# Bilinear feature interaction on one core: w in four loads of 128 rows, x in 16 KB pieces, and another set of x blocks on fifteen DMA engines

## The chip, the core and the metric

The kernel runs on one core of a Trainium2 chip. The core has a matrix engine (TensorE, PE in the profile; its weight loads are PEld), a vector engine (DVE), a scalar engine (ACT), a general engine (GpSimd, POOL) and a queue engine that only issues transfers (SyncE, SP). Sixteen DMA engines move data between the core's memory and HBM for all of them. The metric is the device time of one execution in microseconds (us). Lower is better.

## The reference

Each of 4096 samples has 32 fields of 64 numbers. For each of the 496 pairs of fields i < j, field i is multiplied by the pair's own 64 x 64 matrix, and the result by field j, element by element:

```python
B, F, D = (4096, 32, 64)
idx_i, idx_j = np.triu_indices(F, k=1)
vi = inputs[:, idx_i, :]
vj = inputs[:, idx_j, :]
vidots = jnp.einsum('bpd,pde->bpe', vi, W)
return vidots * vj            # (4096, 496, 64) float32
```

The output has 520 MB, the input x 33.6 MB and the weights W 8.1 MB, so nearly all traffic is the output.

## The kernel before

**Tiling.** The samples form 16 blocks of 256. A block's x lies in one tile `xs`: 128 partitions, each with two samples (k = 0 and 1) of 32 x 64 floats, 8 KB a sample. Half a block (128 samples, one k) is a unit t of work, 32 in all. The pairs are cut into five groups (`bounds`, L45), and one output tile `ot` holds one unit's results of one group, 2880 to 3360 KB. There are three `ot` buffers (`opool`, L58), two `xs` buffers (`xpool`, L55) and four PSUM buffers.

**Steps.** For a unit, `turn_x` (L148) transposes eight fields at a time on PE, and ACT copies them out of PSUM in three pieces (L158 to L160). For each i, up to 16 pairs are one step: two matmuls, one for each half of the columns (L254), then a multiply with field j into `ot`, on DVE straight from PSUM (L274), or, for the seven i in `aside` (L49), a copy by ACT (L271) and the multiply on POOL (L272). When a group is full, SP issues the output transfer (L279). The first three units go through the groups together (`LEAD`, L178), later units one after the other.

**Weights.** W is loaded as it lies, one pair to a partition (16 KB), in the parts `wrows` (L51, L52): 128, 128, 128 and 112 pairs. `order_w` (L130) reorders a quarter of a part (DVE, for part 2 POOL, for half of part 3 ACT), `turn_w` (L139) transposes it, and the result lies in a tile `wT`: one for the first three parts, one for the last (`home_of`, L114). Parts 0 and 1 are loaded into `ot` buffers, part 2 into its own place in `wT`, part 3 into the later home of part 3. A step whose pairs lie across the border of the two homes has its matmuls split there (L250).

**Loads.** SP issues, in this order: half of block 0, w parts 0 and 1, the other half of block 0, block 1, w parts 2 and 3 (L205 to L213). After that SP's queue carries outputs alone. Block b + 1 is loaded while block b is worked on (`loads`, L202). A plain load (`load_x`) is one transfer from ACT's queue. Every third block (3, 6, 9, 12, 15; L231) goes from GpSimd's queue instead, through `load_fifteen` (L95): first 120 of the 128 partitions in one transfer, then the other 8 partitions in two transfers of half the fields each. GpSimd's queue gives a transfer of few rows to a run of DMA engines that starts where the one before ended; `turn_engines` (L86) are tiny transfers that move this start: by 5 at the beginning, by 1 between the parts of each such load, by 11 at the end. So 120 partitions go to fifteen engines, always the same fifteen, and the 8 + 8 pieces of the rest to all sixteen once.

**Layout of xs.** `new_x` (L69) leaves 16 floats between the two samples of a partition, so that every x transfer moves pieces of 8 KB.

Of the kernel before, what the change touches and what calls it, by code (L numbers as in the profile page):

```python
# [8 lines left out]
F32 = mybir.dt.float32  # L9
# [3 lines left out]
def kernel(  # L13
# [16 lines left out]
    nc = tc.nc  # L30

    B, F, D = x.shape
    P = 128
    NB = 2
    assert 2 * D == P and B % (NB * P) == 0
    NBLK = B // (NB * P)
    NP = F * (F - 1) // 2
# [10 lines left out]

    aside = (1, 3, 5, 7, 9, 11, 13)  # L49

    cuts = [*range(0, NP, P), NP]  # L51
    wrows = list(zip(cuts[:-1], cuts[1:]))  # L52

    const = ctx.enter_context(tc.tile_pool(name="const", bufs=1))
    xpool = ctx.enter_context(tc.tile_pool(name="xpool", bufs=2))  # L55
# [8 lines left out]
    xs = {}  # L64

    def rows_of(dram: bass.AP, blk: int) -> bass.AP:
        return dram[blk * NB * P : (blk + 1) * NB * P]

    def new_x(blk: int):  # L69

        wide = xpool.tile([P, NB, F * D + 16], F32, tag="xs", name=f"xs_{blk}")
        xs[blk] = wide[:, :, : F * D].rearrange("p k (f d) -> p k f d", d=D)

    def load_x(blk: int, eng, k0: int = 0, k1: int = NB):
        src = rows_of(x, blk).rearrange("(p k) f d -> p k f d", k=NB)
        eng.dma_start(out=xs[blk][:, k0:k1], in_=src[:, k0:k1])
# [18 lines left out]
    def load_fifteen(blk: int):  # L95
        rows = rows_of(x, blk).rearrange("(p k) f d -> p k f d", k=NB)
        dst = xs[blk]

        def part(ps: slice, fs: slice):
            tc.keep_in_program_order(nc.gpsimd.dma_start(out=dst[ps, :, fs, :], in_=rows[ps, :, fs, :]))  # L100

        part(slice(0, SWR), slice(0, F))
        turn_engines(1)
        for h in range(2):
            part(slice(SWR, P), slice(h * F // 2, (h + 1) * F // 2))


    wflat = w.rearrange("p d e -> p (d e)")
    raw, wT = {}, {}
    EU = 2 * BANK // P  # L110
    NU = E2 // EU


    def home_of(c: int):  # L114
        home, tag, n = (wrows[3][0], "w3", NP - wrows[3][0]) if c == 3 else (0, "w", wrows[3][0])
        if home not in wT:
            wT[home] = const.tile([P, n, E2], F32, tag=tag, name=f"wT_{home}")
        return wT[home][:, wrows[c][0] - home : wrows[c][1] - home, :]

    def load_w(c: int):  # L120

        a, b = wrows[c]
        if c == 2:
            raw[c] = home_of(c).rearrange("p r e -> p (r e)")
        else:
            pool, tag = (const, "w3") if c == 3 else (opool, "ot")
            raw[c] = pool.tile([P, D * D], F32, tag=tag, name=f"raw_{c}")
        nc.sync.dma_start(out=raw[c][: b - a, :], in_=wflat[a:b])  # L128

    def order_w(c: int, k: int, copy):  # L130
        r = wrows[c][1] - wrows[c][0]
        rp = tpool.tile([P, EU, 2, D], F32, tag="tmp", name=f"rp_{c}_{k}")
        src = raw[c][:r, :].rearrange("p (d h e) -> p e h d", h=2, d=D)
        ins = copy(rp[:r], src[:, k * EU : (k + 1) * EU])  # L134
        if c > 0:
            tc.keep_in_program_order(ins)
        return rp

    def turn_w(c: int, k: int, rp, copy):  # L139
        r = wrows[c][1] - wrows[c][0]  # L140
        pt = psum.tile([P, EU, P], F32, tag="ps", name=f"ptw_{c}_{k}")
        for n in range(EU):
            nc.tensor.transpose(  # L143
                pt[:, n, :r], rp[:r, n].rearrange("p h d -> p (h d)"), ident[:r, :r]
            )
        copy(home_of(c)[:, :, k * EU : (k + 1) * EU], pt[:, :, :r].rearrange("p e r -> p r e"))  # L146

    def turn_x(blk: int, k: int, q: int, copy):  # L148


        pt = psum.tile([P, RUN // 2, P], F32, tag="ps", name=f"ptx_{blk}_{k}_{q}")
        for u in range(RUN // 2):
            f = q * RUN + 2 * u
            nc.tensor.transpose(  # L154
                pt[:, u, :], xs[blk][:, k, f : f + 2, :].rearrange("p f d -> p (f d)"), ident
            )
        xT = xtpool.tile([P, 2, RUN // 2, P], F32, tag="xT", name=f"xT_{blk}_{k}_{q}")
        copy(xT[:, 0], pt)  # L158
        copy(xT[D:, 1], pt[:D])  # L159
        copy(xT[:D, 1], pt[D:])  # L160
        return xT
# [40 lines left out]
    loads = {place[blk * NB, LATE]: blk + 1 for blk in range(2, NBLK - 1)}  # L202
    loads[place[LEAD, LATE]] = 2

    new_x(0)  # L205
    load_x(0, nc.sync, 0, 1)
    load_w(0)
    load_w(1)
    load_x(0, nc.sync, 1, NB)
    new_x(1)  # L210
    load_x(1, nc.sync)
    load_w(2)
    load_w(3)  # L213
    turn_engines(5)

    v, p, a = nc.vector.tensor_copy, nc.gpsimd.tensor_copy, nc.scalar.copy
# [5 lines left out]
    for k, copy in ((0, a), (3, a), (1, v), (2, a)):  # L222
        turn_w(0, k, rps.pop((0, k)), copy)

    ots = {}
    for s, (t, st) in enumerate(sched):
        blk, kt = divmod(t, NB)
        g, i, c0, m = steps[st]
        if s in loads:
            new_x(loads[s])  # L230
            if loads[s] % 3 == 0:  # L231
                load_fifteen(loads[s])
            else:
                load_x(loads[s], nc.scalar)
        for what, *args in due.get(s, ()):
            if what == "x":
                xT[tuple(args)] = turn_x(*args, a)
            elif what == "turn":
                turn_w(*args, rps.pop(tuple(args)), a)
            else:  # L240
                c, k = args
                rps[c, k] = order_w(c, k, ((v, v, p, v), (v, v, p, a))[k % 2][c])

        base, end = groups[g]
        pa = p0[i] + c0
        if pa == base:
            ots[t] = opool.tile([P, cap, D], F32, tag="ot", name=f"ot_{t}_{g}")
        ot = ots[t]
        ps = psum.tile([P, 2, CH, E2], F32, tag="ps", name=f"ps_{s}")
        for lo, hi in ((0, wrows[3][0]), wrows[3]):  # L250
            home, lo, hi = lo, max(pa, lo), min(pa + m, hi)
            if lo < hi:
                for h in range(2):
                    nc.tensor.matmul(  # L254
                        ps[:, h, lo - pa : hi - pa, :],
                        xT[blk, kt, i // RUN][h * D : (h + 1) * D, (i + h) % 2, i % RUN // 2, :],
                        wT[home][h * D : (h + 1) * D, lo - home : hi - home, :],
                        start=True,
                        stop=True,
                    )  # L260
        o = pa - base
        j = i + 1 + c0
        dst = ot[:, o : o + m, :].rearrange("p m (h e) -> p m h e", h=2)
        src = ps[:, :, :m, :].rearrange("p h m e -> p m h e")
        xj = xs[blk][:, kt, j : j + m, :].rearrange("p m (h e) -> p m h e", h=2)
        if i in aside and c0 == 0:

            tmp = dst
            if t >= LEAD:
                tmp = tpool.tile([P, CH, 2, E2], F32, tag="tmp", name=f"tmp_{s}")  # L270
            nc.scalar.copy(tmp, src)  # L271
            nc.gpsimd.tensor_mul(dst, tmp, xj)  # L272
        else:
            nc.vector.tensor_mul(dst, src, xj)  # L274

        ends = (p0[2], end) if s < NS and (t, g) == (0, 0) else (end,)
        if pa + m in ends:
            n0 = p0[2] if len(ends) > 1 and pa + m == end else base
            nc.sync.dma_start(  # L279
                out=rows_of(out, blk).rearrange("(p k) n d -> p k n d", k=NB)[:, kt, n0 : pa + m, :],  # L280
                in_=ot[:, n0 - base : pa + m - base, :],
            )
# [28 lines left out]
```

## Time and profile before

| | |
|---|---|
| time, median of 3 | 1338.6 us (1338.33 to 1338.76) |
| span of the profiled execution | 1337.1 us |
| HBM read, written | 41.68 MB, 520.09 MB |
| DMA queue of SP / ACT / GpSimd | 532.43 / 18.87 / 10.50 MB |
| share of 16 engines' time, same order | 93.9% / 3.4% / 2.0% |
| output transfers | 161, median 15.6 to 17.0 us from issue to landing by size (most of them) |
| x, plain, from ACT: 9 | 25.4 us from issue to landing |
| x, 120 rows, from GpSimd: 5 | 24.8 us |
| x, 8 rows, from GpSimd: 10 | 28.2 us |
| last part of w, 112 rows: 1 | 30.3 us |
| DVE waits for an output buffer | 210.7 us in 101 waits, longest 5.5 |
| POOL waits for an output buffer | 173.9 us in 65 waits, longest 5.3 |

The time from issue to landing contains the time in the queue behind earlier transfers. An engine that waits for an `ot` buffer waits for the landing of the transfer that last read it. DMA shares are the packets' time over the time of all 16 engines, so one busy engine alone has a share of 0.06. A share can come out a little over 1, because a packet is counted where it starts.

### The profile page before, as it was taken

What the parts mean: (1) busy time and instruction counts of PE and PEld (TensorE: products, weight loads), DVE (VectorE), ACT (ScalarE), POOL (GpSimd) and SP (SyncE); (2) the same over time, 40 slices, a digit from 0 to 9 for tenths busy, and PEclk for the clock granted to TensorE, in tenths of its full rate; (3) what the DMA queues carried; (4) which work ended last, traced back from release to release, by engine and by line L of the source; (5) the groups of instructions that cost most, each with busy time, mean ns of one, the idle gap of its engine ahead of it and who ended that gap; (6) DMA issues with size and microseconds to landing.
All of it is one profiled execution on the core that took longest, in us unless ns stands there. A gap on an engine that the chain in (4) does not pass through costs nothing.

```text
span 1337.1 us, 16689 instructions
## 1 busy us (share of the span) xinstructions
PE 1134.5 (85%) x6656; PEld 604.6 (45%) x6656; DVE 952.7 (71%) x1258; ACT 471.4 (35%) x627; POOL 552.4 (41%) x256
## 2 busy tenths in 40 slices
PE   6989898978798897898888898788897979879884
PEld 4555444444444444444444444444444444444442
DVE  5778677766677676776767777577775767767774
ACT  4463333333233333333333333333333323333331
POOL 1752443344334343343453334444344424444431
PEclk9999899989899898998998989899998999989997
DMA  9999999999999999999999999999999999999997
GB/s 371 431 429 425 426 420 429 423 428 431 424 429 420 421 430 423 431 420 427 432 407 430 424 431 425 422 426 405 429 426 428 426 418 427 422 415 430 430 429 318
DMA packets 28894, 562.86 MB, mean 421 GB/s; under 512 B 3536, under 2 KB 3536, under 8 KB 3824
## 3 DMA queue, kind: packets, MB, share of 16 engines
q1 hardware_dynamic: 24304, 532.43, 93.9%
q10 hardware_dynamic: 2448, 18.87, 3.4%
q0 software_dynamic: 2064, 10.50, 2.0%
q8 instruction: 52, 0.85, 0.2%
q14 instruction: 26, 0.21, 0.0%
HBM read 41.68 MB, written 520.09 MB: 420 GB/s over the span
## 4 chain that ended last, share of the span: by engine, by line
DMA 53%; PE 24%; DVE 14%; POOL 4%; issue 2%; ACT 2%; DVEq 0%; SPq 0%; POOLq 0%; ACTq 0%
DMA out_dram<-ot 52%; PE ps L254 22%; DVE ot L274 13%; POOL ot L272 4%; PE ptx L154 2%; DMA xs<-in_r_inputs_dram 1%; PE ptw L143 1%; ACT tmp L271 1%; DVE rp L134 0%; ACT xT L160 0%; ACT xT L158 0%; ACT xT L159 0%; DVEq L274 0%; POOL xs L100 0%; SPq L128 0%
## 5 line engine op out<-in xcount | busy, mean ns | idle before, releaser
L274 DVE TENSOR_TENSOR ot<-ps,xs 128x1024 f32<-128x1024 f32 (+15 forms) x1248 | 937.7, 806 | 353.3 <-DMA out_dram<-ot 210.7
L254 PE MATMUL ps<-wT,xT 64*128 64x512 f32 (+13 forms) x6016 | 1044.8, 488 | 169.3 <-DVE ot L274 164.5
L254 PEld LDWEIGHTS ps<-wT,xT 64*128 64x128 f32 x6016 | 535.1, 196 | 618.9 <-DVE ot L274 372.5
L272 POOL TENSOR_TENSOR ot<-tmp,xs 128x1024 f32<-128x1024 f32 x203 | 478.9, 2359 | 705.7 <-ACT tmp L271 532.5
L271 ACT COPY tmp<-ps 128x1024 f32<-128x1024 f32 x203 | 205.5, 1012 | 475.7 <-PE ps L254 432.5
L158 ACT COPY xT<-ptx 128x512 f32<-128x512 f32 x128 | 74.9, 585 | 322.5 <-PE ptx L154 322.5
L154 PE MATMUL ptx<-ident,xs 128*128 128x128 f32 x512 | 84.4, 288 | 9.7 <-DMA xs<-in_r_inputs_dram 6.5
L154 PEld LDWEIGHTS ptx<-ident,xs 128*128 128x128 f32 x512 | 53.9, 141 | 81.9 <-DVE ot L274 56.3
L160 ACT COPY xT<-ptx 64x512 f32<-64x512 f32 x128 | 74.5, 582 | 1.5
L159 ACT COPY xT<-ptx 64x512 f32<-64x512 f32 x128 | 73.9, 577 | 1.5
L272 POOL TENSOR_TENSOR ot<-ot,xs 128x1024 f32<-128x1024 f32 x21 | 49.8, 2377 | 51.0 <-ACT ot L271 49.9
L271 ACT COPY ot<-ps 128x1024 f32<-128x1024 f32 x21 | 21.3, 1013 | 24.7 <-PE ps L254 17.1
L143 PE MATMUL ptw<-ident,rp 128*128 128x128 f32 (+1 forms) x128 | 18.4, 297 | 5.8 <-DVE rp L134 5.8
L134 DVE COPY rp<-raw 128x1024 f32<-128x1024 f32 (+1 forms) x9 | 14.7, 1653 | 10.7 <-DMA raw<-in_L_rec_W_dram 10.7
L143 PEld LDWEIGHTS ptw<-ident,rp 128*128 128x128 f32 (+1 forms) x128 | 15.6, 155 | 13.8 <-DVE rp L134 5.2
L146 ACT COPY wT<-ptw 128x1024 f32<-128x1024 f32 (+1 forms) x15 | 14.8, 985 | 12.2 <-PE ptw L143 10.9
L100 POOL DMA_DIRECT2D xs<-in_r_inputs_dram x15 | 9.5, 636 | 0.0
L134 POOL COPY rp<-wT 128x1024 f32<-128x1024 f32 x4 | 7.8, 1967 | 0.0
L134 ACT COPY rp<-raw 112x1024 f32<-112x1024 f32 (+1 forms) x3 | 6.0, 1996 | 1.9 <-DMA raw<-in_L_rec_W_dram 1.9
L92 POOL DMA_DIRECT2D scratch<-in_r_inputs_dram x7 | 6.2, 889 | 0.3 <-issue 0.3
L146 DVE COPY wT<-ptw 128x1024 f32<-128x1024 f32 x1 | 1.2, 1223 | 3.1 <-PE ptw L143 3.1
L158 ACT ACT_TABLE_LOAD x1 | 1.3, 1283 | 0.7 <-PEq L298 0.7
(6 smaller groups left out, 0.9 us busy)
## 6 DMA issues: line engine op xcount, KB each, us to landing
out_dram<-ot SPq DMA_DIRECT2D x64, 3360.0 KB, 16.6
out_dram<-ot SPq DMA_DIRECT2D x32, 3168.0 KB, 15.6
out_dram<-ot SPq DMA_DIRECT2D x32, 3104.0 KB, 17.0
out_dram<-ot SPq DMA_DIRECT2D x31, 2880.0 KB, 16.9
xs<-in_r_inputs_dram ACTq DMA_DIRECT2D x9, 2048.0 KB, 25.4
xs<-in_r_inputs_dram POOLq DMA_DIRECT2D x5, 1920.0 KB, 24.8
raw<-in_L_rec_W_dram SPq DMA_DIRECT2D x2, 2048.0 KB, 11.7
xs<-in_r_inputs_dram SPq DMA_DIRECT2D x2, 1024.0 KB, 10.5
```

Source lines behind the costliest of these rows:

```text
L100: tc.keep_in_program_order(nc.gpsimd.dma_start(out=dst[ps, :, fs, :], in_=rows[ps, :, fs, :]))
L134: ins = copy(rp[:r], src[:, k * EU : (k + 1) * EU])
L143: nc.tensor.transpose(pt[:, n, :r], rp[:r, n].rearrange("p h d -> p (h d)"), ident[:r, :r])
L146: copy(home_of(c)[:, :, k * EU : (k + 1) * EU], pt[:, :, :r].rearrange("p e r -> p r e"))
L154: nc.tensor.transpose(pt[:, u, :], xs[blk][:, k, f : f + 2, :].rearrange("p f d -> p (f d)"), ident)
L158: copy(xT[:, 0], pt)
L159: copy(xT[D:, 1], pt[:D])
L160: copy(xT[:D, 1], pt[D:])
L254: nc.tensor.matmul(ps[:, h, lo - pa : hi - pa, :], xT[blk, kt, i // RUN][h * D : (h + 1) * D, (i + h) % 2, i % RUN // 2, :], wT[home][h * ...
L271: nc.scalar.copy(tmp, src)
L272: nc.gpsimd.tensor_mul(dst, tmp, xj)
L274: nc.vector.tensor_mul(dst, src, xj)
```

## The change

It has three parts.

1. *w.* The parts of w are now pairs 0 to 127, 128 to 255, 256 to 367 and 368 to 495, and each is loaded by a transfer of 128 rows; the third carries 16 rows that the fourth loads too. All four transfers then have eight rows for each DMA engine. The 112 wide part is now part 2 (POOL's), and the border of the two homes is at pair 368 instead of 384.
2. *x pieces.* The gap between a partition's two samples is kept only for blocks that go by fifteen engines. In all others the 16 KB of a partition lie together, and the transfer moves one piece for each partition. The first block, loaded half by half, keeps 8 KB pieces.
3. *Which blocks.* Blocks 5, 7, 9, 11, 13, 14 and 15 are loaded by fifteen engines, where 3, 6, 9, 12 and 15 were. Seven loads leave the sixteenth engine out instead of five, and the first comes later.

```diff
-    cuts = [*range(0, NP, P), NP]
+    cuts = [0, P, 2 * P, NP - P, NP]
     wrows = list(zip(cuts[:-1], cuts[1:]))
...
+    fifteen = (5, 7, 9, 11, 13, 14, 15)
+
     def new_x(blk: int):
-
-        wide = xpool.tile([P, NB, F * D + 16], F32, tag="xs", name=f"xs_{blk}")
+        gap = 16 if blk in fifteen else 0
+        wide = xpool.tile([P, NB * (F * D + 16)], F32, tag="xs", name=f"xs_{blk}")
+        wide = wide[:, : NB * (F * D + gap)].rearrange("p (k n) -> p k n", k=NB)
         xs[blk] = wide[:, :, : F * D].rearrange("p k (f d) -> p k f d", d=D)
...
-    def home_of(c: int):
-        home, tag, n = (wrows[3][0], "w3", NP - wrows[3][0]) if c == 3 else (0, "w", wrows[3][0])
+    def home_of(c: int, r: int):
+        home, tag, n = (wrows[3][0], "w3", P) if c == 3 else (0, "w", 3 * P)
...
-        return wT[home][:, wrows[c][0] - home : wrows[c][1] - home, :]
+        return wT[home][:, wrows[c][0] - home : wrows[c][0] - home + r, :]
 
     def load_w(c: int):
 
-        a, b = wrows[c]
+        a = wrows[c][0]
         if c == 2:
-            raw[c] = home_of(c).rearrange("p r e -> p (r e)")
+            raw[c] = home_of(c, P).rearrange("p r e -> p (r e)")
...
-        nc.sync.dma_start(out=raw[c][: b - a, :], in_=wflat[a:b])
+        nc.sync.dma_start(out=raw[c], in_=wflat[a : a + P])
...
-            if loads[s] % 3 == 0:
+            if loads[s] in fifteen:
                 load_fifteen(loads[s])
```

More of the change, by code (lines that the diff above doesn't have):

```diff
@@ L145, in turn_w @@
             )
-        copy(home_of(c)[:, :, k * EU : (k + 1) * EU], pt[:, :, :r].rearrange("p e r -> p r e"))
+        copy(home_of(c, r)[:, :, k * EU : (k + 1) * EU], pt[:, :, :r].rearrange("p e r -> p r e"))
     def turn_x(blk: int, k: int, q: int, copy):
```

## The prediction

> **What bounds the kernel now.** I read the page first: busy shares, DMA row, queues, chain of waits.
>
> ```profile
> PE 1134.5 (85%) x6656; PEld 604.6 (45%) x6656; DVE 952.7 (71%) x1258; ACT 471.4 (35%) x627; POOL 552.4 (41%) x256
> ...
> DMA  9999999999999999999999999999999999999997
> ...
> DMA packets 28894, 562.86 MB, mean 421 GB/s; under 512 B 3536, under 2 KB 3536, under 8 KB 3824
> ...
> DMA 53%; PE 24%; DVE 14%; POOL 4%; issue 2%; ACT 2%; DVEq 0%; SPq 0%; POOLq 0%; ACTq 0%
> ```
>
> No compute engine is above 85%, the DMA row is full in every slice but the last, and over half of the chain that ended last is the output transfer. So the 16 DMA engines are the bound, and the question is whether all 16 work all the time. The view by stretches of time answers it (columns: stretch, length, busy us of PE, PEld, DVE, ACT, POOL, clock, DMA share, GB/s):
>
> ```profile
> 27.00:34.00 7.00, 7.00 (x42) 3.67 (x38) 6.63 (x7) 3.49 (x5) 2.18 (x1) 1.00 1.01 298
> ...
> 1329.00:1331.00 2.00, 0.00 (x0) 0.00 (x0) 0.00 (x0) 0.00 (x0) 0.00 (x0) 0.50 0.06 27
> 1331.00:1333.00 2.00, 0.00 (x0) 0.00 (x0) 0.00 (x0) 0.00 (x0) 0.00 (x0) 0.50 0.06 27
> ```
>
> A share of 0.06 is one engine of 16: after 1329 us a single DMA engine still writes while fifteen have nothing left. The trace also holds the 16 completion events of every transfer, one per engine (the printed views show only the last). In the last output transfer the fifteen land at 1329.2 on average and the last at 1335.35; the span ends 1.75 later. I call this distance (6.2 us here) the **lag**. It is built up, not an accident of the end: from 3.39 us (transfer issued at 1184.2) to 6.56 (issued at 1310.8), a stretch with no x load, so 0.025 us per us. Over a plain x load it hardly moves (4.54 to 4.82 across block 13's, 980.7 to 1011.4). Over a fifteen-engine load it falls: 6.12 to 2.46 (block 6), 6.95 to 3.38 (block 12), 7.00 to 3.39 (block 15). So the engine left out is the lagging one.
>
> The lag also costs time before the end. An output buffer is free when the last engine has landed, there are three of them, and one transfer takes about 7.7 us; at a lag near 7 us the fast engines run dry. The stretches around x loads show it:
>
> ```profile
> 174.00:214.00 40.00, 33.52 (x198) 17.38 (x196) 27.78 (x39) 14.06 (x19) 19.31 (x11) 0.96 1.01 422
> 252.00:292.00 40.00, 32.38 (x184) 17.33 (x186) 26.17 (x37) 12.45 (x17) 14.89 (x7) 0.91 1.01 422
> ...
> 910.00:950.00 40.00, 34.05 (x200) 17.77 (x197) 27.51 (x38) 14.06 (x19) 19.34 (x11) 0.96 0.98 407
> ...
> 1156.00:1196.00 40.00, 33.66 (x198) 17.38 (x194) 27.41 (x38) 14.06 (x19) 19.34 (x11) 0.96 0.99 408
> ```
>
> The first is a fifteen-engine load at a lag of 3.7, the second a plain one: both 422 GB/s. The last two are fifteen-engine loads that began at a lag of 7: 407 and 408. Adding up, in the packet records from 20 to 1320 us, the time in which fewer than 16 packets were in flight gives 50 us of engine time, 3.1 us per engine.
>
> **What the Trainium skill says.** "DMA: Bandwidth & Descriptors" bears on it in three places. Its section on latency and other measured facts says that engines 7 and 15 are usually slower and suspects the descriptor rings of the GpSimd path. The trace agrees that one engine is slow, but the lag grows from 1200 to 1300 us with no GpSimd transfer in flight, so that cause doesn't carry it here. The section on why a semaphore counts 16 says that a GpSimd transfer runs on consecutive engines from a round-robin cursor, or on ceil(rows/16) rows per engine; either way 120 rows leave one engine out, and each load's 15+1+8+8 = 32 turns bring the cursor back. The falls of the lag above agree. The section on where 436 GB/s comes from gives a ceiling of 435; the best stretches here show 438, so between x loads (429 from 1200 to 1300) there is little left but balance.
>
> **The change, part by part.**
>
> *Two more fifteen-engine loads (7 for 5).* For the lagging engine each takes 8 rows of two 8 KB pieces off, 16 x 0.309 = 4.9 us, and gives back its share of the last 8 rows (two 4 KB pieces of 0.16 us) and the 17-row cursor turn, whose price on that engine I can't see. Measured, the lag falls by 3.6 us where a plain load adds 0.2: 3.8, of which 0.3 to 0.7 was the fast engines running dry. I take 3.3 us of relief per load; the ends are 2.5 (block 3's fall, 3.74 to 1.59, plus 0.2, where another engine may have become last) and 5.1 (the sum of pieces, with what the others take over). For the other fifteen each such load adds the 8 spread rows (0.32 us) and GpSimd pieces averaging 0.324 for 0.309 us (16 x 0.015 = 0.24): 0.55 each, 1.1 for two.
>
> *Which blocks.* Before, relief comes at 185, 431, 676, 922 and 1167 us; after, near 342, 505, 676, 833, 996, 1079 and 1167. Without the one at 185 the lag at 342 is about 5.6 + 2.5 to 3.3, minus 1.5 from w below: 7, just where the engines run dry; I allow 0.3 us. From then a pair of blocks (164 us) adds about 120 x 0.025 + 0.2 = 3.2 against 3.3 of relief, so the lag peaks near 7 and then lower, and blocks 14 and 15 bring it near zero or below; the last 160 us add some 3 again. The fast engines' 3.1 us of running dry all but go.
>
> *x in 16 KB pieces.* In the packet records an 8 KB piece takes 0.309 and a 16 KB piece 0.611 us: 0.007 saved per pair, 8 pairs per engine and load, 8 loads (block 1 and seven): 0.4 us on every engine. The x load gets more of the engines while it runs, so outputs then land later, but three buffers hold work for that.
>
> *w by 128 rows.* From 27 to 34 us the DMA share is 1.01 at 298 GB/s: full engines, slow pieces (0.8 to 1.0 us for the 112-row part against 0.611). The transfer has 7 pieces per engine, and the first landings of the two w parts are 6.5 us apart; 8 pieces at 0.611 are 4.9. Gain 1.5 us, the 0.26 MB more included. But from 60 to 110 us the chain is PE and DVE: the output issued at 90.4 leaves the queue only 1.5 us of slack, and the engines run dry for a moment there. So the fast engines give the gain back as idle time; the lagging one, with work queued, keeps it. I count 0 for the fifteen and 1.5 off the lag. The 112 rows that go through POOL instead of ACT or DVE, and the split of a matmul at pair 368 instead of 384, cost nothing: counts are the same, and the copies are per column.
>
> *POOL* gets two more groups of four issues (three of 0.64, one of 0.89): 2.8 us each, hidden in its 705.7 us idle before multiplies (532.5 of that waiting for ACT); what queues behind is a multiply, and the output waited 26.6 us in all for POOL. *ACT* loses two issues of 0.56, also hidden.
>
> Sum: fifteen engines finish at 1329.2 - 3.1 + 0.3 + 1.1 - 0.4 = 1327.1. The lag at the end is 6.2 + 3.1 - 0.3 (no longer shortened by running dry) - 2 x 3.3 - 1.5 = 0.9. End 1328.0, plus 1.75: 1329.8 against a span of 1337.1, so 7.3 us less: **1331.3 us**.
>
> **Rivals.** (a) *Lag remains*: relief only 2.5 and half of w's gain kept: 6.2 + 2.8 - 5.0 - 0.7 = 3.3, plus another engine's stray load (the second-last stands 2 to 4 us behind the mean in mid-run, and is not relieved): some 3.8. End 1327.1 + 3.8 + 1.75 = 1332.7, time 1334.1. For it: block 3's small fall. (b) *w's gain kept by all*: 1.5 less, 1329.8. For it: full engines at 34 us; against it: the slack of 1.5 at 90. (c) *Slower*: the low rates of 407 to 413 GB/s are the price of the GpSimd path itself: 15 GB/s over 40 us is 0.5 MB, 1.2 us, times two; the tail stays, because three loads in the last four blocks are spent on an engine already ahead while the early run is dry, and w's 0.6 us of extra bytes is paid: 1338.6 + 2.4 + 0.6 = 1341.6. Against it: 422 GB/s at 174 us. (d) *No change*: relief and these costs cancel, 1338.
>
> **How the numbers follow.** Forecast 0.55, (a) 0.22, (b) 0.10, (c) 0.07, (d) 0.06. The time is the forecast's. The range takes in (b) and (a) with an error of about 1 us each, 1329 to 1335.3, and leaves 0.13 to (c) and (d) and a little beyond (b). Within 0.2% is 1335.9 to 1341.3: 0.06; faster 0.87; slower 0.07.
>
> **What would show it.** Right: no 0.06 share after the fifteen have landed; the last output's lag at 0 to 2; 420 GB/s or more around all fifteen-engine loads from block 7 on; over 400 GB/s from 27 to 34 us; a 16 KB size for x pieces, fewer packets. Wrong if one engine is still 4 us late at the end, if the late loads stay near 407, or if a stretch without x loads is below 429.

## The result and the profile after

The changed kernel takes 1333.2 us (median of 6 runs, 1331.3 to 1336.2) against 1338.5 beside it: a ratio of 0.9964, with a 95% interval of 0.9951 to 0.9977. That is 5.3 us less, where 7.3 were forecast. The time lies in the stated range, between the forecast (1331.3) and rival (a), *lag remains* (1334.1), and nearer to the rival. The profiled execution is the fastest of the six (1331.3 us, span 1329.5); a second profile of the same kernel (experiment 8) is of 1334.3 us. Both are used below.

The page of the changed kernel, the same rows as before:

```profile
PE 1139.7 (86%) x6656; PEld 605.9 (46%) x6656; DVE 950.9 (72%) x1258; ACT 471.7 (35%) x627; POOL 558.4 (42%) x264
...
DMA  9999999999999999999999999999999999999998
...
DMA packets 28142, 563.13 MB, mean 424 GB/s; under 512 B 3760, under 2 KB 3760, under 8 KB 4112
...
DMA 55%; PE 19%; DVE 15%; POOL 4%; issue 4%; ACT 1%; DVEq 0%; POOLq 0%; SPq 0%; ACTq 0%
```

The engines work as long as before, 0.27 MB more are moved, and the mean rate rises from 421 to 424 GB/s. The DMA engines are still the bound. Where they gained shows in the stretches (stretch, length, busy us of PE, PEld, DVE, ACT, POOL, clock, DMA share, GB/s), those of before again and some more from the start and the end:

```profile
27.00:34.00 7.00, 7.00 (x42) 3.70 (x40) 6.63 (x7) 3.50 (x6) 2.21 (x1) 1.00 1.00 395
...
60.00:80.00 20.00, 16.55 (x94) 8.44 (x91) 16.23 (x17) 13.81 (x15) 12.95 (x6) 0.93 1.01 433
80.00:100.00 20.00, 20.00 (x137) 12.21 (x136) 13.45 (x19) 10.81 (x12) 9.99 (x5) 0.98 0.89 378
...
334.00:374.00 40.00, 35.14 (x205) 18.48 (x204) 29.19 (x40) 14.07 (x19) 19.37 (x11) 0.96 1.00 418
...
910.00:950.00 40.00, 32.73 (x184) 17.18 (x180) 25.65 (x33) 12.32 (x16) 16.53 (x7) 0.91 1.00 425
...
1156.00:1196.00 40.00, 33.10 (x174) 17.63 (x172) 25.85 (x32) 12.32 (x16) 19.30 (x11) 0.88 1.01 418
...
1323.00:1325.00 2.00, 0.00 (x0) 0.00 (x0) 0.00 (x0) 0.00 (x0) 0.00 (x0) 0.50 0.56 242
1325.00:1327.00 2.00, 0.00 (x0) 0.00 (x0) 0.00 (x0) 0.00 (x0) 0.00 (x0) 0.50 0.34 148
1327.00:1329.50 2.50, 0.00 (x0) 0.00 (x0) 0.00 (x0) 0.00 (x0) 0.00 (x0) 0.50 0.03 11
```

Four readings. The load of w runs at 395 GB/s instead of 298. From 80 to 100 us the DMA engines now stand still for a tenth of the time (0.89); in the kernel before it was 1.01:

```profile
80.00:100.00 20.00, 20.00 (x145) 11.82 (x143) 14.09 (x20) 11.56 (x15) 11.24 (x5) 1.00 1.01 430
```

Around the fifteen-engine loads at 350 and 1167 us the rate is 418, where late ones had 407 and 408; around a plain load (910 us) it is 425. And at the end the share falls in steps, 0.56, 0.34, 0.03: several engines finish late together, where one alone (0.06) had worked for 6 us. In the completion events the last output ends 2.9 us after the mean of the other fifteen, and the last but one only 0.1 us before it.

**Who is last.** The trace has every packet's start and length, and an engine's next packet starts 3 or 4 ns before the one before it ends. So the packets of the engine that ends last can be chained backwards. In the kernel before, its output packets in the last 60 us of computing take 34 ns longer on average than the shortest of their size (0.855 to 0.996 us). In both profiles of the changed kernel they take at most 2 ns longer: an ordinary engine ends last. But the slow engine is close behind it in rank. Followed back in the same way, the engine that ends last but one has the stretch: 41 ns on the 11 output packets of computing that its chain holds in the first profile, 35 ns on 42 in the second. It lands 0.1 and 1.2 us before the last one, which is 2.8 and 2.6 us behind the mean of the others. Before, the slow engine was 6.2 us behind.

**After the last landing.** The span of the kernel before ends 1.70 us after its last landing, that of the changed kernel 0.99 and 0.98 us after. In all three profiles with five fifteen-engine loads (before, experiments 2 and 3) it is 1.70 to 1.72 us, and an 8 KB packet of an instruction queue (q14) starts 1.2 us after the last landing. In all eight profiles with seven such loads it is 0.98 or 0.99 us, and that packet starts over 10 us before the last landing. So about 0.7 us of the gain is this shorter end. It goes with where the instruction packet falls, and is not the balance of the engines.

### The profile page after: what moved, and what is told of

It is laid out like the page before. It is cut to its first block, busy times and chain, and to the rows that moved or that the text cites. A ratio compares the mean times of both kernels' runs of the same rounds, so it can differ in the third digit from the quotient of the medians.

```text
span 1329.5 us, 16690 instructions
## 1 busy us (share of the span) xinstructions
PE 1139.7 (86%) x6656; PEld 605.9 (46%) x6656; DVE 950.9 (72%) x1258; ACT 471.7 (35%) x627; POOL 558.4 (42%) x264
## 2 busy tenths in 40 slices
DMA packets 28142, 563.13 MB, mean 424 GB/s; under 512 B 3760, under 2 KB 3760, under 8 KB 4112
## 4 chain that ended last, share of the span: by engine, by line
DMA 55%; PE 19%; DVE 15%; POOL 4%; issue 4%; ACT 1%; DVEq 0%; POOLq 0%; SPq 0%; ACTq 0%
DMA out_dram<-ot 55%; PE ps L259 17%; DVE ot L279 15%; POOL ot L277 4%; PE ptx L159 1%; POOL rp L139 1%; ACT tmp L276 0%; DMA xs<-in_r_inputs_dram 0%; PE ptw L148 0%; DVE rp L139 0%; DVEq L279 0%; ACT xT L163 0%; ACT xT L164 0%; ACT xT L165 0%; POOLq L277 0%
## 5 line engine op out<-in xcount | busy, mean ns | idle before, releaser
L259 PE MATMUL ps<-wT,xT 64*128 64x512 f32 (+12 forms) x6016 | 1049.0, 489 | 157.4 <-DVE ot L279 152.5
L139 DVE COPY rp<-raw 128x1024 f32<-128x1024 f32 x9 | 14.7, 1650 | 10.6 <-DMA raw<-in_L_rec_W_dram 10.6
L151 ACT COPY wT<-ptw 128x1024 f32<-128x1024 f32 (+1 forms) x15 | 14.8, 984 | 13.8 <-PE ptw L148 10.9
L105 POOL DMA_DIRECT2D xs<-in_r_inputs_dram x21 | 13.3, 637 | 0.0
L139 POOL COPY rp<-wT 112x1024 f32<-112x1024 f32 x4 | 7.9, 1978 | 0.0
L139 ACT COPY rp<-raw 128x1024 f32<-128x1024 f32 x3 | 6.0, 1987 | 1.9 <-DMA raw<-in_L_rec_W_dram 1.9
```

The lines of the kernel that those rows point to most:

```text
L151: copy(home_of(c, r)[:, :, k * EU : (k + 1) * EU], pt[:, :, :r].rearrange("p e r -> p r e"))
L259: nc.tensor.matmul(ps[:, h, lo - pa : hi - pa, :], xT[blk, kt, i // RUN][h * D : (h + 1) * D, (i + h) % 2, i % RUN // 2, :], wT[home][h * ...
```

## The experiments

Each kernel ran beside the kernel before; the ratio is to those runs, in brackets its 95% interval.

**1. The new set of blocks alone** (w as before, all pieces 8 KB):

```diff
-            if loads[s] % 3 == 0:
+            if loads[s] in (5, 7, 9, 11, 13, 14, 15):
```

> Only the set of blocks is changed (5, 7, 9, 11, 13, 14, 15 on fifteen engines); w keeps its 112-row part and all x pieces have 8 KB. Balance theory (the gain comes from leaving a lagging engine out twice more): nearly the whole gain, 1333 to 1335 us; in the last output the last engine within 4 us of the mean of the others. Rival, w theory (the gain is the faster load of w): 1338, no change. Rival, pieces theory: 1338 to 1339, the lag at the end gone or not, because the GpSimd loads cost as much as they bring.

1335.9 us, 0.9983 [0.9974, 0.9992]: 2.7 us of the 5.3. In its profile the slow engine is still last, 5.8 us behind the mean of the others, its packets stretched by 31 ns. The slow engine lands 3.0 us earlier than before (1332.35 for 1335.35), 1.5 us for each load added. So the set is half of the gain, not nearly all of it, and 0.7 us of that half is the shorter end of the program.

**2. w alone** (the changed kernel with blocks 3, 6, 9, 12, 15 and 8 KB pieces):

> Only the load of w is changed (four times 128 rows). Balance theory: the fifteen fast engines run dry for about 1.5 us near 90 us, where PE and DVE set the pace, and give the gain back; the lagging engine keeps up to 1.5 us, so 1337 to 1338.5. w theory: 1333 to 1335. The rate from 27 to 34 us rises from 298 to about 400 GB/s in both.

1337.5 us, 0.9992 [0.9983, 1.0000]: 1.1 us, inside what was expected of w kept by the slow engine alone, though the interval just reaches no change. Its stretches (columns as above):

```profile
27.00:34.00 7.00, 7.00 (x40) 3.63 (x38) 6.64 (x7) 3.65 (x5) 2.03 (x1) 1.00 1.00 384
60.00:80.00 20.00, 16.50 (x102) 8.86 (x98) 16.82 (x17) 14.17 (x16) 13.11 (x6) 1.00 1.01 432
80.00:100.00 20.00, 20.00 (x139) 11.87 (x140) 13.84 (x20) 11.89 (x14) 11.08 (x5) 1.00 0.95 405
```

Faster at 27 us, idle at 80 to 100 us: with PE busy for all 20 us at full clock, the share is 0.95, so about 1 us on each engine is handed back. The landings show it too. The fifteen land an output at 83.5 us on average where the kernel before had 84.35, but the second one after it at 99.4 where it had 99.55; the slow engine lands that one 1.2 us earlier (100.4 for 101.6).

**3. 16 KB pieces alone** (blocks 3, 6, 9, 12, 15 on fifteen engines, w as before):

```diff
...
+        gap = 16 if blk in (3, 6, 9, 12, 15) else 0
...
```

> Only the plain x loads are changed (16 KB pieces; blocks 3, 6, 9, 12, 15 stay on fifteen engines). By the packet times (0.309 and 0.611 us) 0.6 us less on every engine: 1337.5 to 1338.2. Pieces theory: 3 us or more less, 1335.5 or lower, with a higher rate around the plain loads than the 422 to 425 GB/s of before.

1338.5 us, 1.0001 [0.9993, 1.0009]: no change that can be measured.

**4. Another engine left out** (the changed kernel, with the turns of GpSimd's start moved):

```diff
-    turn_engines(5)
+    turn_engines(13)
...
-    turn_engines(11)
+    turn_engines(3)
```

> The changed kernel, with the first turn of GpSimd's start at 13 instead of 5 (and the last at 3 instead of 11): the seven loads leave another engine out. Balance theory with one particular slow engine: the lag is not relieved by any load, the fast engines run dry at a lag near 7 us from about 250 us on, and the end is set by the slow engine: its work grows by the five lost reliefs, 5 x 3.3 = 16, so 1350 to 1358 us, and GB/s falls below 425 between x loads. Rival (any engine left out gives the same, since the load on GpSimd's queue or the spread itself brings the gain): 1333.

1353.5 us, 1.0111 [1.0098, 1.0125], as the balance theory had it. The same seven loads on the same queue, only with another engine spared, cost 20 us. That another one is spared also shows in the completion events of the 120-row loads: here one engine reports 4.9 to 15.7 us before the next, in the changed kernel at most 2.2 us. The end of its run:

```profile
1344.00:1346.00 2.00, 0.00 (x0) 0.00 (x0) 0.00 (x0) 0.00 (x0) 0.00 (x0) 0.50 0.06 27
1346.00:1348.00 2.00, 0.00 (x0) 0.00 (x0) 0.00 (x0) 0.00 (x0) 0.00 (x0) 0.50 0.06 27
1348.00:1350.00 2.00, 0.00 (x0) 0.00 (x0) 0.00 (x0) 0.00 (x0) 0.00 (x0) 0.50 0.06 27
```

One engine works alone again, and from 120 to 1300 us the records show 180 us of engine time without a packet (before 49, changed kernel 10 and 15): the fast engines wait all along.

**5. No load on fifteen engines** (`fifteen = ()`, all plain in 16 KB pieces):

> The changed kernel with no x load on fifteen engines (all plain, 16 KB pieces). Balance theory: the slow engine keeps all x rows; against the kernel that leaves another engine out (1353.5) it is spared seven shares of the spread rows, 7 x 0.55 = 3.9 us: 1349 to 1351, at the end one engine 6 to 7 us behind, and the fast engines dry at a lag near 7 from about 250 us on. Rival (GpSimd's queue itself costs): 1333 to 1336.

1348.1 us, 1.0070 [1.0056, 1.0084]; 1 us less than expected. The last engine is the slow one, 6.2 us behind.

**6. All 13 loads on fifteen engines:**

> The changed kernel with all 13 blocks from 3 on loaded on fifteen engines. Balance theory: the slow engine is far ahead, the other fifteen take over 0.55 us for each of the six further loads, 3.3 us in all: 1335.5 to 1337, and the last engine is one of the fifteen. If more relief were still wanted, 1331 or less.

1338.0 us, 0.9994 [0.9986, 1.0002]: 1 us more than expected. Six loads more than in the changed kernel cost 4.5 to 4.8 us. Of that, 0.7 us is the end of the program, 1.71 us after the last landing as in the kernel before; the rest is 0.6 to 0.7 per load instead of 0.55. The last engine is an ordinary one. The slow engine (14 packets stretched by 40 ns) is not far ahead, as was expected, but 0.8 us behind the mean of the others.

**7. Seven loads, spread evenly** (`fifteen = (3, 5, 7, 9, 11, 13, 15)`), and **8. the changed kernel once more**:

> The changed kernel with the same number of fifteen-engine loads on other blocks, 3, 5, 7, 9, 11, 13, 15 (not 14). Balance theory: the number counts, the place only where the lag comes near 7: the lag at 340 us is 2 to 3 us lower and the 0.6 us of running dry after 120 us goes, so 0 to 1 us less than the changed kernel, 1332 to 1333.5. Rival (the late loads 13, 14, 15 bring the gain): 1335 or more.

> The changed kernel itself, beside the others on one chip, for a second profile. 1331 to 1336 us as before; the lag at the end 0 to 3. If the variation of the start (a lower PE clock between 60 and 100 us) makes the spread of its times, this profile shows either a full clock and under 15 us of idle engine time from 20 to 120 us, or a dip and about 30.

1332.8 us, 0.9955 [0.9943, 0.9968], and 1333.5 us, 0.9961 [0.9949, 0.9974]. The number of loads counts; which blocks, by no more than the noise. The spread set has the lag down to 3.0 us at 308 us (changed kernel 4.9 at 310), and yet, as far as its chain can be followed, it is the slow engine that ends last, 1.2 us after the next, while in the changed kernel, with blocks 14 and 15 late, it is last but one. Running dry after 120 us doesn't go, as was expected of the spread set: 19 us of engine time, for 10 and 15 in the changed kernel.

The start of the second profile of the changed kernel, and of the spread set:

```profile
60.00:80.00 20.00, 16.55 (x96) 8.41 (x92) 15.89 (x16) 14.63 (x17) 13.36 (x6) 0.96 1.00 431
80.00:100.00 20.00, 20.00 (x134) 12.23 (x132) 12.88 (x18) 10.48 (x12) 9.47 (x4) 0.96 0.90 380
```

```profile
60.00:80.00 20.00, 16.54 (x104) 8.94 (x102) 16.93 (x17) 14.05 (x16) 13.08 (x6) 1.00 1.00 428
80.00:100.00 20.00, 20.00 (x140) 11.90 (x142) 13.68 (x20) 12.03 (x15) 11.22 (x5) 1.00 0.99 421
```

With the clock of PE at 0.96 the DMA share is 0.90, with 1.00 it is 0.99: between 20 and 120 us, 41 against 10 us of idle engine time. In this stretch PE sets the pace, and a lower granted clock costs the DMA engines up to 2 us. That this is the clock and not the new w shows in experiment 3: with the old load of w, at a clock of 0.97 and 0.94 from 60 to 100 us, it has 28 us of idle engine time from 20 to 120 us, where the other three kernels with the old w (before, 1 and 9), at full clock, have 2 to 3. It is part of the spread of the times, but not their order: the fastest profile of all (1331.3) also had a dip.

**9. The changed kernel without the new w:**

> The changed kernel with the old load of w (128, 128, 128, 112 rows). Alone, the new load brought 1.1 us. If w's gain is kept by the slow engine alone, as forecast, and the slow engine is still near the end's bound: 1 to 2 us slower than the changed kernel, 1334.5 to 1335.5. If the fifteen fast engines set the end of the changed kernel by a margin: within 0.5 of it, 1333 to 1334.

1335.0 us, 0.9978 [0.9970, 0.9986]: 1.5 to 1.9 us slower than the changed kernel's two medians (the intervals just overlap), and the last engine is the slow one again, 5.5 us behind the mean of the others. So w's gain counts as long as the slow engine sets the end, although the fast engines don't keep it.

**10. The changed kernel with 8 KB pieces everywhere** (`gap = 16`):

> The changed kernel with all x pieces of 8 KB. By the packet times 0.4 to 0.5 us slower than the changed kernel: 1333.5 to 1334.2. If the size of the pieces acts on the slow engine beyond the packet times (the two small parts together brought 2.6 us on top of the new blocks, where alone they bring 1.3): 1335 or more.

1336.6 us, 0.9988 [0.9980, 0.9996]: over 3 us slower than the changed kernel, which neither the packet times nor experiment 3 lets one expect. In its profile an ordinary engine ends last, and the outputs' packets are stretched by 18.0 us per engine in all, against 14.8 and 15.5 in the two profiles of the changed kernel. It also runs dry more, 31 us of engine time from 120 to 1300 us against 10 and 15. Why the outputs are stretched more there, but not in experiment 1 (14.0, also 8 KB), is open.

**11. Six loads on fifteen engines** (3, 5, 8, 10, 13, 15):

> The changed kernel with six fifteen-engine loads, on 3, 5, 8, 10, 13 and 15. Per load taken away the slow engine gets 2.7 us more and the fifteen 0.55 less. If seven is past the balance (the fifteen set the end): 1332 to 1333, no slower than the changed kernel. If the slow engine still sets it: 1335 to 1336.

1334.1 us, 0.9969 [0.9958, 0.9980], between the two expectations. The last engine is the slow one (packets stretched by 34 ns), landing at 1333.1 us; with seven spread loads it landed at 1330.0. The 3.0 us between them are not the worth of one load, since this profile is of the slowest of the seven runs (1335.8 us), and the intervals of the times with six and seven loads overlap. What puts the balance near seven is which engine ends last: with six loads the slow one by 5.0 us, with seven the slow one by 1.2 us or an ordinary one by 0.1 and 1.2 us, with thirteen an ordinary one.

**12. Seven spread loads with 16 KB pieces for GpSimd's queue too:**

```diff
-        gap = 16 if blk in fifteen else 0
+        gap = 0
```

> The kernel with blocks 3, 5, 7, 9, 11, 13, 15 on fifteen engines, and 16 KB pieces for these loads too (no gap anywhere, so that the 120 rows move 16 KB each). Two pieces of 8 KB from GpSimd's queue took 0.316 us on average each, one of 16 KB from ACT's 0.617: 8 x 0.015 = 0.1 us per load and engine from that, and if 16 KB pieces also stretch the outputs beside them less (0.9 to 1.0 us per load now, 0.5 to 0.6 for ACT's 16 KB loads), 0.4 more. Theory that the number of pieces matters: 1329.5 to 1331. Rival (the price is GpSimd's queue): as with 8 KB, 1332 to 1333; more if the lagging engine is relieved less.

1357.3 us, 1.0150 [1.0136, 1.0163]: neither. The rows now form one piece each, the transfer is described with one dimension less, and another engine is left out: in each of the seven loads one engine reports completion 2.7 to 11 us before the rest, much as in experiment 4, while at the end the slow one is last, 6.8 us behind:

```profile
1348.00:1350.00 2.00, 0.00 (x0) 0.00 (x0) 0.00 (x0) 0.00 (x0) 0.00 (x0) 0.50 0.06 27
1350.00:1352.00 2.00, 0.00 (x0) 0.00 (x0) 0.00 (x0) 0.00 (x0) 0.00 (x0) 0.50 0.06 27
```

So the gap of 16 floats is not about the size of pieces: with it, and with the turns of the start, the engine left out is the slow one. It also confirms experiment 4 by another route. Of its rule nothing more was tried.

## Why the prediction was right, point by point

- **The bound and the tail: right.** One slow engine set the end, 6.2 us behind the others; leaving it out oftener brings it to 2.8 and 2.6 us behind them, and it must be this engine: another costs 20 us (4), none 15 us (5).
- **Relief of 3.3 us per load (2.75 of it on the slow engine itself): too large in most of the runs.** The slow engine's last landing goes from 1345.2 (none) to 1333.1 (six), 2.0 per load (2.3 by the medians of the times), and in experiment 1 by 1.5 for each of the two added. Rival (a)'s 2.5, which is 1.95 on the slow engine itself, fits better. In the changed kernel, with w and the pieces, it lands 6.9 and 5.0 us earlier than before, where the sum has 7.4. What takes the rest of the relief away is open.
- **0.55 us per load on the other fifteen: a little small.** Thirteen loads against seven give 0.6 to 0.7, and a rate of 418 for 425 over 40 us is 0.7 us. The sum had no term for what an x load does to the outputs beside it: summed over the output packets while it is under way, they take 0.8 to 0.9 us per engine longer for a GpSimd load, 0.5 for a plain 16 KB load (changed kernel), 0.65 for a plain 8 KB load (kernel before). In all this did not make the changed kernel slower: its outputs are stretched by 14.8 and 15.5 us per engine, those of the kernel before by 16.2.
- **Running dry: right.** From 120 to 1300 us the idle engine time falls from 49 us to 10 and 15, so from 3.1 us per engine to 0.6 and 0.9; 0.3 was allowed. From 20 to 120 us it rises instead, from 2 us to 30 and 41; that belongs to the next point.
- **w: right in mechanism.** Given back by the fast engines between 80 and 100 us, kept by the slow one; 1.1 us alone, 1.5 to 1.9 in the changed kernel, 1.5 forecast. The rate at 27 us, 395 and 379 in the two profiles, is short of the 400 asked for. What the step did not have is that this stretch hangs on PE's clock: at 0.93 to 0.98 the engines stand still for about 2 us, not 1.5.
- **16 KB pieces, 0.4 us: open.** Alone not measurable (3), in the changed kernel 3 us (10). The working by packet times describes the first and not the second. Rival (d), in which nothing is gained, is refuted all the same.
- **The lag at the end, 0.9 us: the step that was off.** It is 2.9 and 3.9. The slow engine itself is still 2.8 and 2.6 us behind the mean of the others: in the second profile for want of relief, in the first mainly because the others are early. The engine that ends last is an ordinary one, for which the sum had no term. Rival (a) had both: less relief (3.3 of lag) and a stray load of another engine (3.8).
- **That the sum came out so near in the first profile is luck.** There the fifteen ended at 1325.6, 1.5 us earlier than forecast, and the span ended 0.99 us after the last landing, where 1.75 was carried over from the kernel before. Together this hid the 2 us of lag too many (span 1329.5 for 1329.8). In the second profile the fifteen ended at 1327.6, 0.5 later than forecast; the lag, 3.0 too large, was made up for by 0.8 at the end alone, and the span is 1332.5.
- **Its own signs: mostly not met.** No engine works alone for long, and the packets are fewer (28142 for 28894). But the lag is not 0 to 2, the rate around fifteen-engine loads is 418 and not 420, the load of w is under 400 GB/s, and in the second profile 1200 to 1300 us has 427 GB/s, under the 429 that was named.
- **Rival (b), w's gain kept by all: wrong** (idle at 80 to 100 us in 2). **Rival (c), slower: wrong**, although its premise is partly true: a GpSimd load does cost the others more than a plain one. (Its 15 GB/s over 40 us are 0.6 MB or 1.4 us, not 0.5 and 1.2; nothing hangs on it.)

## What to carry to other kernels

When the DMA row is full everywhere, look at the last microseconds: a share of 1/16 for some time means that one engine carries more or is slower, and its distance from the mean of the others is what balance can win. In this kernel, sparing it was worth doing only for the engine concerned and only up to the point where ordinary engines end last; each further load cost all others. Compare the time after the last landing as well: part of a small gain can lie there. A faster load at the start gained nothing on the engines that ran dry later in the start, where a compute engine set the pace.

## What the runs showed of the hardware that was not expected

The slow DMA engine was seen to be slow only while the core computes. In the kernel before and in experiments 1, 4, 5, 9, 11 and 12 its output packets take 30 to 34 ns longer than the shortest of their size in the last part of computing (58 packets each, 56 us), and from about 2 us after the last multiply on mostly 0 and at most 16 ns longer, though the other fifteen engines still write for another 7 us then; in five of these seven runs a single packet of that time stands out, by some 270 ns: it comes right after an 8 KB packet of an instruction queue (q14) on this engine. The Trainium skill, in the table of latency and other measured facts of "DMA: Bandwidth & Descriptors", looks for the cause in the descriptor rings of the GpSimd path; here the stretch is seen on SP's outputs between the GpSimd loads as well, and without any such load, but for the two tiny turns of GpSimd's start, in experiment 5. What in the computing slows this one engine was not tried.

Fetching instructions costs an ordinary DMA engine more than the fetch itself. A run has 52 packets of 16 KB on an instruction queue (q8), of 0.94 us each on average, and the output packet that follows one on the same engine takes some 0.4 us longer than the shortest of its size (median 399 to 409 ns in every profile, 27 to 38 such pairs found in each). Whether this is what sets the ordinary engines apart at the end (their last landings lie 5.0 us apart in the first profile) was not tried.

From 27 to 34 us, with a transfer of 112 rows among those of w, the engines are busy at a lower rate: 293 to 304 GB/s at a share of 0.99 to 1.02 (before, 1, 3 and 9), against 377 to 395 with 128 rows in each (all others).

A GpSimd transfer of the same 120 rows leaves out one engine or another according to how the rows are described, which changed the time by 24.5 us (1357.3 against 1332.8).
